# Layer 3 of a four-layer graph network: where the next batch's norm stands in VectorE's queue, and which block computes the first one

## The chip, the cores and the metric

The kernel runs on one core of one Trainium2 chip. The metric is the device time of one execution in microseconds (us). An execution is profiled once; it has a span, from its first to its last instruction, and some time around it.

## What is computed

Four layers share a residual: each takes h = relu(layernorm(x)) over 256 features, and adds its own result to x. Inputs are x (16 x 1024 x 256 values) and adj (16 x 1024 x 1024), in float32, read by the layers in other shapes of the same numbers. Layers 0 and 1 are dense graph layers. Layer 2 is a recurrence over nodes, which the kernel runs for all 16 batches at once. Layer 3, which the change is mostly about, is, cut to what matters:

```python
h = jnp.maximum(_layernorm(x, axis=-1), 0.0)
neighbor_sum = jnp.einsum('bnm,bmd->bnd', adjacency, h)
agg = epsilon * h + neighbor_sum
y = jnp.einsum('bnd,dh->bnh', agg, W1) + b1            # 256 -> 1024
y = jax.nn.silu(_rmsnorm(y, rms_weight))
out = jnp.einsum('bnh,hd->bnd', y, W2) + b2            # 1024 -> 256
x = x + out
```

## The kernel before

The names: a batch (b, 16 of them) has 1024 rows in 8 tiles of 128 (NT = 8), 256 features in two halves of 128 (DC = 2), 1024 hidden features in 8 pieces (HC = 8). Everything is float32.

Layers 0 and 1 run batch after batch and leave x in DRAM (x2_d). Layer 2 (layer_2, line 562 and on) walks over t = 0 to 7, one tile of 128 nodes of all 16 batches, and within it over s = 0 to 7, sub-steps of 16 nodes. A sub-step takes x from bxt and near (L970), runs round_ (L802 the matmuls, L843 and on the gates), turns the result (L870, L873) into h, and writes h with two indirect DMAs from GpSimd's queue to hs_d, one for each group of eight batches (L1034). Behind each sub-step stands a branch (tc.If, L1018) with repeats of the round for long chains of nodes. The recurrence is a chain: each sub-step needs the one before. In layer 2 the order of the instructions of TensorE, VectorE, ScalarE and GpSimd is the order in which the program writes them (manual_schedule); other work of the same block (L637, L687, L784, L749) is put between by hand. DMA issues of SP's queue are placed by the scheduler.

Before its last block, t = 7, the kernel calls early() (L919), which is early_3 (L1056): it starts the loads of batch 0 of layer 3: x[0], the first half of the transposed adjacency at[0][0], and the rows hn[0] of layer 2's result for tiles 0 to 6. They go into buffers of the pool "shared", which has two buffers of the name hb (x[0] and hn[0]) and two of the name bxt.

Layer 3 (layer_3, L1067) is not ordered by hand: a scheduler places the instructions of each engine at build time by the data they need and the buffers that are free, and may put later lines of the program ahead of earlier ones. For each batch there are these steps:

- load(b), L1093: x[b] (three buffers), hn[b] (layer 2's result, 7 tiles from hn_d and the last from hs_d; the two hb buffers), and at[b] in two halves of 512 columns, each in four pieces. Even batches use the two bxt buffers, odd ones two buffers named at. All are issued on SP's queue, which is first in, first out.
- prepare(b), L1108: GpSimd adds epsilon on the diagonal of at (L1112, four tiles for each half, with eye = epsilon times the unit matrix, L1088). VectorE adds hn[b] to x[b] (L1117, all eight tiles in one instruction but for batch 0) and calls ln_relu (L86): statistics for each tile (L92, L93), variance plus a constant (L79), GpSimd's power of -1/2 (L83), then for each tile VectorE's (x - mean) * rs into h[b] (L96) and ScalarE's Relu on it (L98). GpSimd adds b2 to x[b] (L1121). For batch 0 this is done in three parts, tiles 0 to 3, 4 to 6 and 7.
- sums(b), L1123: four parts of eight matmuls (L1130), one for each half of at and each half of the features; ScalarE or VectorE copies each result to ag (L1133, L1135). There are two pa buffers in PSUM.
- inner(ag, n0), L1138, for each half of the rows: for each of 8 pieces two matmuls into ph (L1145, two ph buffers in PSUM), ScalarE's square (L1148), VectorE's copy with b1 to hh (L1149), GpSimd's sum of the squares ss (L1151).
- norm: mean (L1163, four small matmuls, then L81 and L83), spread (L1169, four transposes into pr), apply (VectorE's hh * pr at L1174, ScalarE's Silu at L1175).
- outer(b, hh, n0), L1178: for each of four tiles eight matmuls into po (L1183, two po buffers) and VectorE's addition to x[b] (L1186).

A trace shows two matmul records for each float32 matmul of the program. The loop over batches at the end of layer_3 interleaves them: inner for both halves of b, two parts of sums(b + 1), outer for the first half, the third part of sums, prepare(b + 2), the fourth part, outer for the second half, and the output's DMA (L1217) from GpSimd's queue. prepare(b + 2) is written behind the third part, but in the built program the scheduler has put VectorE's part of it among the evictions of inner of the same batch b, for b = 2 to 13.

Of the kernel before, what the change touches and what calls it, by code (L numbers as in the profile page):

```python
# [40 lines left out]
def gnn_stack(ctx: ExitStack, tc: tile.TileContext, a: dict, out: bass.AP):  # L41
# [30 lines left out]
    def rows(ap):  # L72
        return ap.rearrange("(t p) d -> p t d", p=P)

    def inv_sqrt(pool, src, eps, shape, name, mul=1.0):
# [8 lines left out]
        return r  # L84

    def ln_relu(small, h, x):  # L86

        n = x.shape[1]
        mv = small.tile([P, NT, 2], F32, name="mv")
        for t in range(n):  # L90
            st = small.tile([P, 6], F32, name="st", bufs=4)
            nc.vector.bn_stats(st, x[:, t])  # L92
            nc.vector.bn_aggr(mv[:, t], st)  # L93
        rs = inv_sqrt(small, mv[:, :n, 1], LN_EPS, [P, n], "rs")
        for t in range(n):
            nc.vector.tensor_scalar(h[:, t], x[:, t], mv[:, t, 0:1], rs[:, t : t + 1],  # L96
                                    op0=ALU.subtract, op1=ALU.mult)
            nc.scalar.activation(h[:, t], h[:, t], AF.Relu)  # L98

# [462 lines left out]
    def layer_2(shared, early):  # L562
        with ExitStack() as st:
# [334 lines left out]
            with tc.manual_schedule(engines={mybir.EngineType.PE, mybir.EngineType.DVE, mybir.EngineType.Activation, mybir.EngineType.Pool}):  # L898
# [18 lines left out]
                for t in range(NT):  # L917
                    if t == NT - 1:
                        early()  # L919
                    base_todo = deque()  # L920
# [7 lines left out]
                    for s in range(NS):  # L928
# [68 lines left out]
                        for k, cut in enumerate(CUTS.get(s, ())):  # L997
# [11 lines left out]
                            if last:  # L1009
                                rx = round_(dx, xs, rx, cut, None, rest_if(False, 1.3), hT)  # L1010
                                turned(hT, rest_if(True, 0.5), h)
                            else:
                                rx = round_(dx, xs, rx, cut, hT, rest_if(False, 1.3), changes[cut])
                                dh = work.tile([P, G2, D], F32, name="dh", bufs=1)
                                turned(changes[cut], rest_if(False, 0.5), dh)
                                nc.gpsimd.tensor_tensor(from_(hT, cut), from_(hT, cut), from_(changes[cut], cut), ALU.add)
                        in_arms = gx.tasks if gx and s > 0 else ()
                        with tc.If(n_more[0][s] > 0, preferred_fallthrough_block=False) as more_or_not:  # L1018
# [25 lines left out]
                        elif t + 1 < NT:  # L1044
# [3 lines left out]
                            bxt, he = bxt_next, he_next  # L1048
                        sub = sub_next


# [3 lines left out]

    def early_3(shared, x, hn, at):  # L1056

        x[0] = shared.tile([P, NT, D], F32, name="hb")
        nc.sync.dma_start(x[0], rows(x2_d[0]))
# [4 lines left out]
        nc.sync.dma_start(hn[0][:, : NT - 2], rows(hn_d[0])[:, : NT - 2])  # L1064
        nc.sync.dma_start(hn[0][:, NT - 2], hs_d[NT - 2][0][:P])

    def layer_3(shared, x, hn, at):  # L1067
        with ExitStack() as st:
# [3 lines left out]
            psum = st.enter_context(tc.tile_pool(name="psum3", bufs=2, space=PSUM))  # L1072

            w1 = wp.tile([P, DC, H], F32, name="w1")
            nc.sync.dma_start(w1, a["W1"].rearrange("(c p) e -> p c e", p=P))
# [8 lines left out]
            nc.sync.dma_start(b2, bcast_row(a["b2"], D))  # L1084
            eps = wp.tile([P, 1], F32, name="eps")
            nc.sync.dma_start(eps, bcast_row(a["epsilon"], 1))
            eye = wp.tile([P, P], F32, name="eye")
            nc.vector.tensor_scalar(eye, ident, eps, None, op0=ALU.mult)  # L1088

            NH = 512  # L1090
            h = {}

            def load(b):  # L1093
                if b:
                    x[b] = big.tile([P, NT, D], F32, name="x", bufs=3)
                    nc.sync.dma_start(x[b], rows(x2_d[b]))
                    hn[b] = shared.tile([P, NT, D], F32, name="hb")
                    nc.sync.dma_start(hn[b][:, : NT - 1], rows(hn_d[b])[:, : NT - 1])
                    at[b] = []
                nc.sync.dma_start(hn[b][:, NT - 1], hs_d[NT - 1][b // GB][b % GB * P : (b % GB + 1) * P])  # L1100
                while len(at[b]) < N // NH:
# [6 lines left out]
            def prepare(b):  # L1108
                def diagonal(half):
                    for t in range(half * NT // 2, (half + 1) * NT // 2):  # L1110
                        own = at[b][half][:, t, t * P % NH : t * P % NH + P]
                        nc.gpsimd.tensor_tensor(own, own, eye, ALU.add)  # L1112
                diagonal(0)
                h[b] = big.tile([P, NT, D], F32, name="h", bufs=2)
                for part in ((0, NT),) if b else ((0, 4), (4, NT - 1), (NT - 1, NT)):
                    part = slice(*part)
                    nc.vector.tensor_add(x[b][:, part], x[b][:, part], hn[b][:, part])  # L1117
                    ln_relu(small, h[b][:, part], x[b][:, part])
                diagonal(1)
# [58 lines left out]
            def outer(b, hh, n0, apply=None):  # L1178
                for k in range(NH // P):
# [15 lines left out]
            for b in range(B):  # L1195
# [24 lines left out]
    with tc.tile_pool(name="shared", bufs=2) as shared:  # L1220
        x, hn, at = {}, {}, {}
        layer_2(shared, lambda: early_3(shared, x, hn, at))
        layer_3(shared, x, hn, at)

# [45 lines left out]
```

## Time and profile before

| what | us |
|---|---|
| median of three runs (4855.44 to 4871.58) | 4860.91 |
| the profiled execution | 4861.04 |
| its span | 4858.2 |
| TensorE busy with matmuls | 4494.9 (93%) |
| VectorE busy | 2303.1 (47%) |
| first matmul of layer 3 (L1130) starts at | 3418.39 |
| first ph matmul (L1145) of batch 0 starts at | 3447.76 |
| first ph matmul of batch 1 starts at | 3542.76 |

Times of single instructions are counted from the span's start. A row of the timeline gives start, length, engine, line, operation, output and inputs, how many instructions it merges, and in square brackets how long the engine stood idle before them and what ended that. A row of groups gives after the first bar the busy time and the mean length of one in ns, after the second bar the idle time just before them and what ended most of it. A row of the chain of waits gives start, length and what the path went through; "issue" is time in which nothing shown was waited for. PE is TensorE, DVE VectorE, ACT ScalarE, POOL GpSimd, SP the engine that issues most DMAs. A name in a row is the program's name of the buffer; batch 0's x and hn have the name hb.

### The profile page before, as it was taken

How to read it: one execution, taken by the hardware profiler on the slowest of the kernel's cores; microseconds unless marked ns; L12 is line 12 of the kernel's file. 1: busy time of each engine (PE TensorE's matmuls, PEld its weight loads, DVE VectorE, ACT ScalarE, POOL GpSimd, SP SyncE). 2: the span in 40 equal slices, each digit the busy share in tenths (PEclk: the TensorE clock that was granted, in tenths of full speed). 3: DMA queues.
4: the chain of work that ended last, by engine and by line, in shares of the span. 5: the costliest groups of instructions: out<-in, count | busy, mean ns of one | idle time of the engine just before them, and what ended most of it. 6: DMA issues, size and time to landing. Idle time of an engine off the chain costs nothing. (4 is left out here: it accounts for less than half of the span.)

```text
span 4858.2 us, 52472 instructions
## 1 busy us (share of the span) xinstructions
PE 4494.9 (93%) x18199; PEld 3004.6 (62%) x18199; DVE 2303.1 (47%) x6354; ACT 1220.2 (25%) x2629; POOL 1586.6 (33%) x1939
## 2 busy tenths in 40 slices
PE   8998899999997999999999999998899999999999
PEld 4443455555555777777777777776455555555556
DVE  6667854455543444444444444454534344344342
ACT  1211112222212222222322222222223223223232
POOL 3223233343323322332232323331534234243231
PEclk9999999999998999999999999998899999999999
DMA  4333235555537444444344544420422231222100
GB/s 157 113 99 104 88 88 183 194 165 176 184 104 209 149 137 133 149 142 149 115 140 122 157 139 153 142 82 29 169 87 70 78 104 65 91 88 78 70 26 18
DMA packets 530978, 576.61 MB, mean 119 GB/s; under 512 B 42544, under 2 KB 439472, under 8 KB 528304
## 3 DMA queue, kind: packets, MB, share of 16 engines
q1 hardware_dynamic: 499536, 460.27, 30.6%
q0 software_dynamic: 31040, 111.44, 6.4%
q8 instruction: 197, 3.23, 0.3%
q14 instruction: 205, 1.68, 0.1%
HBM read 469.65 MB, written 116.65 MB: 121 GB/s over the span
## 5 line engine op out<-in xcount | busy, mean ns | idle before, releaser
L309 PE MATMUL pa<-at,h 128*128 128x512 f32 x1088 | 497.4, 610 | 32.9 <-DVE ag L314 32.9
L1145 PE MATMUL ph<-ag,w 128*128 128x512 f32 x1024 | 478.3, 609 | 32.7 <-DVE hh L1149 32.4
L1183 PE MATMUL po<-w,hh 128*128 128x256 f32 x2048 | 447.7, 379 | 0.0
L637 PE MATMUL pf<-hb,ab 128*128 128x256 f32 x1568 | 420.6, 387 | 29.0 <-DVE bxt L787 16.2
L1183 PEld LDWEIGHTS po<-w,hh 128*128 128x128 f32 x2048 | 387.8, 190 | 59.3 <-issue 7.9
L309 PE MATMUL pa<-at,q 128*128 128x512 f32 x960 | 424.2, 595 | 0.0
L309 PEld LDWEIGHTS pa<-at,h 128*128 128x128 f32 x1088 | 209.9, 196 | 278.5 <-issue 232.8
L749 PE MATMUL pf<-hs,wx 128*128 128x256 f32 x1536 | 351.1, 383 | 16.6 <-POOL hs L740 14.9
L1145 PEld LDWEIGHTS ph<-ag,w 128*128 128x128 f32 x1024 | 178.6, 189 | 294.0 <-DVE hh L1149 151.4
L1151 POOL TENSOR_TENSOR ss<-ss,sq 128x512 f32<-128x512 f32 x224 | 304.9, 1361 | 118.7 <-ACT sq L1148 114.3
L749 PEld LDWEIGHTS pf<-hs,wx 128*128 128x128 f32 x1536 | 292.1, 192 | 60.1 <-POOL hs L740 16.8
L637 PEld LDWEIGHTS pf<-hb,ab 128*128 128x128 f32 x1568 | 278.2, 192 | 69.5 <-DVE bxt L787 23.4
L309 PEld LDWEIGHTS pa<-at,q 128*128 128x128 f32 x960 | 178.2, 190 | 216.1 <-issue 212.6
L1149 DVE TENSOR_SCALAR hh<-ph,b 128x512 f32<-128x512 f32 x256 | 189.8, 746 | 153.8 <-ACT sq L1148 120.5
L784 PE MATMUL pf<-bd,h 128*128 128x384 f32 (+5 forms) x768 | 214.4, 373 | 51.7 <-DVE bxt L787 26.5
L1034 POOL DMA_INDIRECT hs_d<-h,table x128 | 129.3, 1010 | 365.4 <-ACT gates L757 179.7
L1130 PE MATMUL pa<-bxt,h 128*128 128x512 f32 x512 | 227.9, 597 | 18.6 <-POOL bxt L1112 18.6
L1130 PE MATMUL pa<-at,h 128*128 128x512 f32 x512 | 228.8, 597 | 0.0
L1148 ACT ACTIVATE sq<-ph,b 128x512 f32<-128x512 f32 x224 | 153.6, 686 | 233.6 <-PE ph L1145 188.2
L787 DVE TENSOR_TENSOR bxt<-bxt,pf 128x384 f32<-128x384 f32 (+5 forms) x384 | 141.2, 384 | 149.1 <-PE pf L784 146.6
L1175 ACT ACTIVATE hh<-hh,rw 128x512 f32<-128x512 f32 x256 | 168.4, 712 | 138.5 <-DVE hh L1174 136.5
L754 DVE TENSOR_TENSOR gates<-pf,bias 128x512 f32<-128x512 f32 x128 | 88.4, 691 | 227.3 <-PE pf L749 227.3
(253 smaller groups left out, 7318.6 us busy)
## 6 DMA issues: line engine op xcount, KB each, us to landing
at<-in_adjT SPq DMA_DIRECT2D x64, 1024.0 KB, 7.2
ab<-in_adj SPq DMA_DIRECT2D x128, 512.0 KB, 4.0
bxt<-in_adjT SPq DMA_DIRECT2D x64, 512.0 KB, 5.8
at<-in_adjT SPq DMA_DIRECT2D x64, 512.0 KB, 5.8
ad<-in_adj SPq DMA_DIRECT2D x128, 128.0 KB, 6.0
x_d<-x POOLq DMA_DIRECT2D x16, 1024.0 KB, 5.4
he_d<-h POOLq DMA_DIRECT2D x16, 1024.0 KB, 9.5
heT_d<-hT POOLq DMA_DIRECT2D x16, 1024.0 KB, 4.4
```

The lines of the kernel that those rows point to most:

```text
L309: nc.tensor.matmul(pa, h[:, mt, c * P : (c + 1) * P], at[n0 // 512][:, mt], start=mt == 0, stop=mt == NT - 1)
L637: nc.tensor.matmul(pb, ab[:, jts[k]], hb[:, jts[k]], start=k == 0, stop=k == len(jts) - 1)
L749: nc.tensor.matmul(pg[:, e], wx[:, c, q * D + e * P : q * D + (e + 1) * P], self.hs[:, c], start=c == 0, stop=c == DC - 1)
L784: nc.tensor.matmul(pf, h[:, g, c * P : (c + 1) * P], bd[:, g, b4 : b4 + 4, S : S + far], start=True, stop=True)
L787: return lambda: nc.vector.tensor_add(to, to, pf)
L1130: nc.tensor.matmul(pa, h[b][:, mt, c * P : (c + 1) * P], at[b][n0 // NH][:, mt], start=mt == 0, stop=mt == NT - 1)
L1145: nc.tensor.matmul(ph, w1[:, c, k * P : (k + 1) * P], ag[:, c, n0 : n0 + NH], start=c == 0, stop=c == DC - 1)
L1148: nc.scalar.activation(sq, ph, AF.Square, bias=b1[:, k : k + 1])
L1149: nc.vector.tensor_scalar(hh[:, k], ph, b1[:, k : k + 1], None, op0=ALU.add)
L1151: nc.gpsimd.tensor_tensor(ss, ss, sq, ALU.add)
L1175: nc.scalar.activation(hh[:, k], hh[:, k], AF.Silu, scale=rw[:, k : k + 1])
L1183: nc.tensor.matmul(po, hh[:, c, k * P : (k + 1) * P], w2[:, c], start=c == 0, stop=c == HC - 1)
```

## The change

It has two parts.

In the batches of layer 3, prepare(b + 2) stands in a block tc.issue_after(last), where last is the fourth addition of outer's first half: each VectorE instruction of the block is ordered behind that addition. The addition of hn to x goes by two tiles at a time. The normalisation itself moves from VectorE to ScalarE: one small VectorE instruction makes shift = -mean * rs, and ScalarE's Relu takes shift as its bias and rs as its scale. VectorE's pass over each tile (L96) goes. The load of the last tile of hn stands directly behind that of the others.

For batch 0, early_3 becomes a generator whose steps layer_2 runs in its last block t = 7: the loads and that of epsilon ahead of the block; then, in one step each behind the rounds of s = 1, 2, 3 and 4: eye and tiles 0 to 2; tiles 3 to 5; tile 6, rs of the seven tiles and the diagonal of the first half; shift and the Relu of the seven tiles. Its small tiles lie in a pool of their own. h[0] is written into the buffer of hn[0]. Layer 3 starts with the load of tile 7 of hn[0] behind that of W1, and prepares only tile 7 and the second half's diagonal.

```diff
                     if t == NT - 1:
-                        early()
+                        eye = next(early)
...
+                        if t == NT - 1 and s > 0:
+                            next(early, None)
...
-    def early_3(shared, x, hn, at):
+    def early_3(shared, pool, x, hn, at, h):
+        eps = pool.tile([P, 1], F32, name="eps")
+        nc.sync.dma_start(eps, bcast_row(a["epsilon"], 1))
         x[0] = shared.tile([P, NT, D], F32, name="hb")
         nc.sync.dma_start(x[0], rows(x2_d[0]))
         at[0] = [shared.tile([P, NT, 512], F32, name="bxt")]
...
         hn[0] = shared.tile([P, NT, D], F32, name="hb")
         nc.sync.dma_start(hn[0][:, : NT - 2], rows(hn_d[0])[:, : NT - 2])
         nc.sync.dma_start(hn[0][:, NT - 2], hs_d[NT - 2][0][:P])
-
+        eye = pool.tile([P, P], F32, name="eye")
+        yield eye
+        n = NT - 1
+        nc.vector.tensor_scalar(eye, ident, eps, None, op0=ALU.mult)
+        mv = pool.tile([P, n, 2], F32, name="mv")
+        for t in range(n):
+            nc.vector.tensor_add(x[0][:, t], x[0][:, t], hn[0][:, t])
+            st = pool.tile([P, 6], F32, name="st", bufs=4)
+            nc.vector.bn_stats(st, x[0][:, t])
+            nc.vector.bn_aggr(mv[:, t], st)
+            if t % 3 == 2:
+                yield
+        rs = inv_sqrt(pool, mv[:, :, 1], LN_EPS, [P, n], "rs")
+        for t in range(NT // 2):
+            own = at[0][0][:, t, t * P : (t + 1) * P]
+            nc.gpsimd.tensor_tensor(own, own, eye, ALU.add)
+        yield
+        h[0] = hn[0]
+        shift = pool.tile([P, n], F32, name="shift")
+        nc.vector.scalar_tensor_tensor(shift, mv[:, :, 0], -1.0, rs, op0=ALU.mult, op1=ALU.mult)
+        for t in range(n):
+            nc.scalar.activation(h[0][:, t], x[0][:, t], AF.Relu, bias=shift[:, t : t + 1], scale=rs[:, t : t + 1])
+        yield
-    def layer_3(shared, x, hn, at):
+    def layer_3(shared, x, hn, at, h, eye):
...
+            nc.sync.dma_start(hn[0][:, NT - 1], hs_d[NT - 1][0][:P])
...
             def load(b):
                 if b:
...
                     nc.sync.dma_start(x[b], rows(x2_d[b]))
                     hn[b] = shared.tile([P, NT, D], F32, name="hb")
                     nc.sync.dma_start(hn[b][:, : NT - 1], rows(hn_d[b])[:, : NT - 1])
+                    nc.sync.dma_start(hn[b][:, NT - 1], hs_d[NT - 1][b // GB][b % GB * P : (b % GB + 1) * P])
                     at[b] = []
-                nc.sync.dma_start(hn[b][:, NT - 1], hs_d[NT - 1][b // GB][b % GB * P : (b % GB + 1) * P])
                 while len(at[b]) < N // NH:
                     n0 = NH * len(at[b])
                     half = shared.tile([P, NT, NH], F32, name="bxt") if b % 2 == 0 else big.tile([P, NT, NH], F32, name="at")
...
                     for t in range(half * NT // 2, (half + 1) * NT // 2):
                         own = at[b][half][:, t, t * P % NH : t * P % NH + P]
                         nc.gpsimd.tensor_tensor(own, own, eye, ALU.add)
-                diagonal(0)
-                h[b] = big.tile([P, NT, D], F32, name="h", bufs=2)
-                for part in ((0, NT),) if b else ((0, 4), (4, NT - 1), (NT - 1, NT)):
-                    part = slice(*part)
-                    nc.vector.tensor_add(x[b][:, part], x[b][:, part], hn[b][:, part])
-                    ln_relu(small, h[b][:, part], x[b][:, part])
+                part = slice(0 if b else NT - 1, NT)
+                if b:
+                    diagonal(0)
+                    h[b] = big.tile([P, NT, D], F32, name="h", bufs=2)
+                tiles = range(NT)[part]
+                mv = small.tile([P, NT, 2], F32, name="mv")
+                for t in tiles[::2]:
+                    two = slice(t, min(t + 2, NT))
+                    nc.vector.tensor_add(x[b][:, two], x[b][:, two], hn[b][:, two])
+                    for t in range(NT)[two]:
+                        st = small.tile([P, 6], F32, name="st", bufs=4)
+                        nc.vector.bn_stats(st, x[b][:, t])
+                        nc.vector.bn_aggr(mv[:, t], st)
+                n = len(tiles)
+                rs = inv_sqrt(small, mv[:, part, 1], LN_EPS, [P, n], "rs")
+                shift = small.tile([P, n], F32, name="shift")
+                nc.vector.scalar_tensor_tensor(shift, mv[:, part, 0], -1.0, rs, op0=ALU.mult, op1=ALU.mult)
+                for k, t in enumerate(tiles):
+                    nc.scalar.activation(h[b][:, t], x[b][:, t], AF.Relu, bias=shift[:, k : k + 1], scale=rs[:, k : k + 1])
                 diagonal(1)
...
-                    nc.vector.tensor_add(x[b][:, t], x[b][:, t], po)
+                    last = nc.vector.tensor_add(x[b][:, t], x[b][:, t], po)
+                return last.ins
...
-                outer(b, hh0, 0, apply1)
+                last = outer(b, hh0, 0, apply1)
                 parts[2]()
                 if b + 2 < B:
-                    prepare(b + 2)
+                    with tc.issue_after(last):
+                        prepare(b + 2)
                 parts[3]()
                 outer(b, hh1, NH)
```

ln_relu, which only layer 3 called, is removed. The other lines of the diff hand eye and h from function to function.

More of the change, by code (lines that the diff above doesn't have):

```diff
@@ L84, in inv_sqrt @@
         return r
[L86 to L98, printed above, removed]
     base_d = dram.tile([B, P, DC, P], F32, name="base_d")
@@ L1049, in layer_2 @@
                         sub = sub_next
-    def early_3(shared, x, hn, at):
+                return eye
+    def early_3(shared, pool, x, hn, at, h):
+        eps = pool.tile([P, 1], F32, name="eps")
+        nc.sync.dma_start(eps, bcast_row(a["epsilon"], 1))
         x[0] = shared.tile([P, NT, D], F32, name="hb")
@@ L1084, in layer_3 @@
             nc.sync.dma_start(b2, bcast_row(a["b2"], D))
[L1085 to L1088, printed above, removed]
             NH = 512
-            h = {}
             def load(b):
@@ L1220, in gnn_stack @@
     with tc.tile_pool(name="shared", bufs=2) as shared:
-        x, hn, at = {}, {}, {}
-        layer_2(shared, lambda: early_3(shared, x, hn, at))
-        layer_3(shared, x, hn, at)
+        x, hn, at, h = {}, {}, {}, {}
+        with tc.tile_pool(name="first3", bufs=1) as first:
+            eye = layer_2(shared, early_3(shared, first, x, hn, at, h))
+            layer_3(shared, x, hn, at, h, eye)
 def kernel(**inputs):
```

## The prediction

> **What bounds the kernel now.** I read the page first, then TensorE's idle time by line, then TensorE's and VectorE's timelines of one layer-3 batch, then the chain of waits where layer 2 turns into layer 3.
>
> ```profile
> PE 4494.9 (93%) x18199; PEld 3004.6 (62%) x18199; DVE 2303.1 (47%) x6354; ACT 1220.2 (25%) x2629; POOL 1586.6 (33%) x1939
> ...
> L1145 PE MATMUL ph<-ag,w 128*128 128x512 f32 x1024 | 478.3, 609 | 32.7 <-DVE hh L1149 32.4
> ```
>
> TensorE is the bound, and the change removes none of its matmuls, so it can only win TensorE's idle time. 32.4 us of it stand before the ph matmuls, waiting for VectorE's eviction hh. Cut at the first ph matmul of a batch, the stage table (stretch, its length, TensorE busy, clock, DMA share, GB/s) shows in which batches:
>
> ```profile
> 3542.76:3629.16 86.40, 86.31 (x282) 1.00 0.21 73
> 3629.16:3719.30 90.14, 85.69 (x274) 1.00 0.23 82
> 3719.30:4615.32 896.02, 872.48 (x2809) 1.00 0.23 81
> 4615.32:4704.77 89.45, 87.10 (x281) 1.00 0.07 24
> 4704.77:4790.87 86.10, 86.10 (x282) 1.00 0.03 13
> ```
>
> The first row is b = 1, the next three are b = 2 to 13, the last is b = 14. Twelve batches take 1075.61 us, 89.63 each; the two at the edges take 86.40 and 86.10. TensorE has the same matmuls in all; the twelve have a next batch's norm on VectorE among the evictions of hh, the two have none. TensorE and VectorE in one of the twelve:
>
> ```profile
> 4012.01 1.98 PE L1145 MATMUL ph<-ag,w 128*128 128x512 f32 x4 [0.37 <-DVE hh L1149]
> ...
> 4014.97 1.99 PE L1145 MATMUL ph<-ag,w 128*128 128x512 f32 x4 [0.87 <-DVE hh L1149]
> ...
> 4019.78 1.98 PE L1145 MATMUL ph<-ag,w 128*128 128x512 f32 x4 [0.68 <-DVE hh L1149]
> ...
> 4023.06 1.98 PE L1145 MATMUL ph<-ag,w 128*128 128x512 f32 x4 [0.44 <-DVE hh L1149]
> ```
>
> ```profile
> 4011.87 2.39 DVE L96 TENSOR_SCALAR h<-x,mv,rs 128x256 f32<-128x256 f32 x4
> 4014.18 0.74 DVE L1149 TENSOR_SCALAR hh<-ph,b 128x512 f32<-128x512 f32 x1
> 4014.84 1.56 DVE L96 TENSOR_SCALAR h<-x,mv,rs 128x256 f32<-128x256 f32 x2
> ```
>
> Four and two normalisations stand ahead of one eviction each; TensorE, with two ph buffers, stops. At the change of layers the chain shows the second loss:
>
> ```profile
> 3402.06 6.03 DMA hs_d<-h,table
> ...
> 3414.76 2.27 DVE h L96 x3
> 3417.03 0.68 DVE eye L1088
> 3417.70 0.07 issue
> 3417.77 0.58 POOL bxt L1112
> 3418.35 0.04 issue
> 3418.39 29.54 PE pa L1130 x64
> ```
>
> TensorE's last transpose of layer 2 ends at 3399.75; batch 0's sums start 18.64 us later, behind the write of h, the norm, eye and the diagonal.
>
> **What the skill says.** "TensorE: Matmul & The Clock Gate", the section on the array's architecture, says that ScalarE's and VectorE's queues are strictly first in, first out. The lines above agree: an eviction whose ph is ready waits 2.39 us behind normalisations. "ScalarE: Activation LUTs", section What ACT_TABLE_LOAD costs, prices each pointer operand (scale, bias) at about 93 ns over an immediate one; here a 128x256 Relu with immediates takes 415 ns (L98), one with both pointers 589 (below), so 87 each: it agrees. I use 589, and 0.50 us apart in a row (589 less the skill's overlap of 93, an estimate).
>
> ```profile
> L301 ACT ACTIVATE h<-x,shift,rs 128x256 f32<-128x256 f32 x128 | 64.7, 589 | 16.6 <-DVE shift L298 16.6
> ```
>
> **Part 1, layer 3's batches.** The built order of after puts all of prepare(b+2) on VectorE between the 4th and the 5th x addition of outer, for b = 0 to 13. Per batch 8 normalisations at 0.648 = 5.2 us go from VectorE; ScalarE's 8 Relu at 0.415 become 8 at 0.589; one tiny shift (0.16) is added. ph's matmuls now run 20, 6, 4, 2 with mean and spread between, as b = 1 and 14 do today, and VectorE's list there is that of b = 1. So I take 86.25 (mean of the two) for all fourteen: 12 x (89.63 - 86.25) = **40.6 us gained**. Bounds: 36 (0.4 us per batch left) to 42.4 (all at 86.10).
> Cover in the new place, on the clock of the batch above: the 4th x addition ends at 4051.8. VectorE then needs 4 additions of two tiles (2.34 in one piece at L1117, so about 2.5), statistics 3.4 (3426.47 to 3429.83 for batch 1), rs_v 0.2; GpSimd's pow 1.65 and two hand-overs 0.3; shift 0.2: done near 4060.2. Queued behind shift are the ag copy, whose pa is ready at 4065.1, and outer's second half, first due 4068.4. Nothing waits. On ScalarE one Relu now stands before the ag copy of 4058.26, which slips to about 4061; its reader is the next batch at 4078. The other seven end near 4065, in 22 us of idle time. GpSimd's x + b2 (8 x 0.77) and four diagonals end near 4073, before the out DMA (4079.66). If that cover were gone, each us of lateness beyond the slack costs 14 us in all.
> DMAs: on SP's queue hn[b+3] now stands between the two halves of at[b+3] and waits for prepare(b+2)'s additions. It lands in 5.1 us after issue, some 80 us before use; x[b+2], issued at 3995.00, is used at 4052. Cost nothing.
>
> **Part 2, batch 0 ahead of time.** In after, tiles 0 to 6, eye, and the first half's diagonal are done in t = 7. The built order of TensorE is 7 matmuls of one sum, 2 of the next, then the one with tile 7. They start when the last h copy is read out, 3400.5 (was 3418.4). 32 matmuls took 29.53 us, 0.92 each, so 9 end at 3408.8. Tile 7: the write of group 0 is issued at 3400.77. In t = 7 such writes land after 2.5 to 2.8 us; here the write of group 1 took 6.03 beside w1 and w2. In after only w1 runs beside it, so I take 4.5: 3405.3. Its load, moved ahead of w2, takes 2.4 to 3: 3408. Addition, statistics, rs_v 1.2, pow 0.6 + 0.2, shift 0.2, Relu 0.6: 3410.7. Stall 1.9 (0 to 6.5). The sums end at 3400.5 + 29.5 + 1.9 = 3431.9 against 3447.9: **16.0 gained** (11.5 to 17.9).
> What is late next is batch 1. h[0] now lies in hn[0]'s buffer, so hn[1] loads only after batch 0's sums (before: issued 3418.05): 3432 + 5.1, and with more behind it about 3437.5. VectorE's two additions for x[1] stand behind two evictions; behind them stand the third eviction and all later ones. Additions and statistics 5.9, so the third eviction is at 3443.3 to 3444.0; TensorE, done with four ph at 3439, idles 5.0. Then 8 Relu (4.0) before the fifth square on ScalarE: idle 4.1; GpSimd's x + b2 (6.1) before the squares' sums: 1.1 more. 10.2 in all over an undisturbed 86.3, so 96.5. Batch 0 took 3542.76 - 3447.76 = 95.0 with its own stalls: **1.5 lost** (4 gained to 7 lost).
>
> **Part 3, layer 2's last block.** Before, two of these additions stand in its first sub-step:
>
> ```profile
> 3207.40 0.96 DVE L1117 TENSOR_TENSOR hb<-hb 128x768 f32<-128x768 f32 x1 [5.40 <-DMA hb<-hs_d]
> 3209.34 2.78 PE L802 MATMUL pc<-r,wh 128*128 128x256 f32 x8 [2.43 <-DVE r L844]
> ```
>
> VectorE waits for a DMA with r behind it, TensorE for r: 2.43, and 0.40 for x behind the first addition: **2.8 gained** (0 if other fillers eat it). Added: in s = 1 and 2 three tiles (0.42 + 0.40 + 0.16 each, 2.9) and eye (0.74), in s = 3 one tile. VectorE idles 2.97 us there in s = 1, 3.04 in s = 2, until the gates' sums; up to 0.7 over, before the second gate eviction, with 0.97 of idle behind it. ScalarE's 7 Relu in s = 4 (3.6) delay a gate eviction by 2; TensorE reads its result over 2 us later. GpSimd's pow and four diagonals (2.8) in s = 3 delay the write of h, whose reader is far. I take nothing, up to 3.
>
> **Sum.** 40.6 + 16.0 - 1.5 + 2.8 = 57.9. The profiled execution took 4861.0 (span 4858.2 and 2.8 around it), within 0.2 us of the median 4860.9. 4861 - 58 = **4803**.
>
> **Rivals.** (a) The change of layers gives little: hn[1] lands late, tile 7 lands after 6 us, the recurrence pays 3: 40.6 + 11.5 - 7 - 3 + 0 = 42, so 4819. For it: VectorE's queue is blocked by a load there for the first time. Against: five us of slack counted already. (b) The stalls don't go with the norm: only VectorE's multiplications by pr hold ph back. Then 16.0 - 1.5 + 2.8 = 17 remains: 4844. For it: 0.68 and 0.44 of the four waits stand among those multiplications. Against: b = 1 and 14 have them too and no wait. (c) Slower: shift waits for GpSimd's pow, which stands behind four diagonals that wait for at[b+2]; today GpSimd waits 101.6 us for at loads (18 times, longest 28.6). The slack to the third po is 4071.4 - 4060.2 = 11 us; each us beyond costs 14, so above 11 + 58/14 = 15 us it is slower than before. At 20 us late: 9 x 14 = 126 - 58, so 4929. Against: in after's order those diagonals are on a half loaded a batch earlier.
>
> **How the numbers follow.** My forecast 0.75, (a) 0.14, (b) 0.06, (c) 0.03, more gain than all the bounds 0.02. All best: 42.4 + 17.9 + 4 + 2.8 = 67, so 4794; (a) reaches 4819, and with 36 in place of 40.6 for the batches 4824. 0.3% is 14.6 us, about what a measurement of this kernel can tell from no change. (b)'s 17 lies just above it, half of it counted as no change: faster 0.94, same 0.03, slower 0.03.
>
> **What would show it.** Right: batches 1 to 14 each near 86.2 us and no [<-DVE hh] waits there; VectorE's shift ahead of the ag copy; batch 0's first sum directly behind layer 2's last transpose; a VectorE wait on hn[1] with TensorE idle near 5 and 4 us behind it. Wrong: batches near 89, TensorE waiting for x additions in outer, a sub-step of t = 7 longer than before.

## The result, and the profile after

The kernel after takes 4802.57 us (median of four runs, 4794.02 to 4806.04) against 4860.06 (four runs, 4855.44 to 4871.58): ratio 0.9872, 95% interval 0.9856 to 0.9888. Its profiled execution took 4804.16, the forecast was 4803.

Of the page after I show the lines that answer to those of before: TensorE's and VectorE's busy time, and the group of the ph matmuls (now L1170), whose idle time <-DVE hh has gone from 32.4 to 8.3 us.

```profile
PE 4482.4 (93%) x18199; PEld 3004.1 (63%) x18199; DVE 2250.0 (47%) x6292; ACT 1238.4 (26%) x2629; POOL 1561.7 (33%) x1938
...
L1170 PE MATMUL ph<-ag,w 128*128 128x512 f32 x1024 | 467.3, 607 | 8.4 <-DVE hh L1174 8.3
```

The stage table, cut at the first ph matmul of a batch: b = 1, b = 2 to 13, b = 14, and last b = 0. Behind the stretch stand its length, then busy time and number of records of TensorE, of its weight loads, of VectorE, ScalarE and GpSimd, then the granted clock, the DMA share and GB/s.

```profile
3529.32:3615.42 86.10, 86.10 (x281) 50.38 (x280) 32.31 (x66) 26.22 (x42) 31.48 (x34) 1.00 0.26 86
3615.42:4648.90 1033.48, 1033.41 (x3362) 604.61 (x3361) 387.62 (x792) 314.64 (x504) 373.41 (x400) 1.00 0.23 80
4648.90:4735.00 86.10, 86.10 (x282) 50.38 (x281) 26.33 (x44) 22.28 (x34) 20.72 (x17) 1.00 0.04 13
3432.51:3529.32 96.81, 88.24 (x281) 51.11 (x280) 39.39 (x88) 31.17 (x51) 41.83 (x50) 0.96 0.38 130
```

TensorE is busy for 1033.41 us of 1033.48: the twelve batches take 86.12 each and it is idle for 0.07 us in all of them. VectorE in one of them, from outer's fourth addition on:

```profile
4018.58 0.42 DVE L1211 TENSOR_TENSOR x<-x,po 128x256 f32<-128x256 f32 x1 [3.03 <-PE po L1208]
...
4026.60 0.17 DVE L1141 SCALAR_TENSOR_TENSOR shift<-mv,rs 128x8 f32<-128x8 f32 x1 [1.76 <-POOL rs L83]
4032.31 0.69 DVE L1160 COPY ag<-pa 128x512 f32<-128x512 f32 x1 [5.54 <-PE pa L1155]
```

Shift ends 7.8 us behind the addition, and the ag copy behind it still waits 5.54 for TensorE. What is left stands in batch 0. TensorE from the end of layer 2 on:

```profile
3401.66 9.69 PE L1155 MATMUL pa<-bxt,hb 128*128 128x512 f32 x18 [0.79 <-ACTq L1008]
3412.66 20.01 PE L1155 MATMUL pa<-bxt,hb 128*128 128x512 f32 x46 [1.31 <-ACT hb L1143]
3432.51 7.14 PE L1170 MATMUL ph<-ag,w 128*128 128x512 f32 x16
3446.08 5.46 PE L1170 MATMUL ph<-ag,w 128*128 128x512 f32 x8 [6.43 <-DVE hh L1174]
3451.38 1.02 PE L1155 MATMUL pa<-at,h 128*128 128x512 f32 x2
3454.26 7.31 PE L1170 MATMUL ph<-ag,w 128*128 128x512 f32 x16 [1.86 <-DVE hh L1174]
```

VectorE in the same time: two evictions, then batch 1's addition, which waits for the load of hn[1], and only behind the statistics the third eviction.

```profile
3436.86 0.75 DVE L1174 TENSOR_SCALAR hh<-ph,b 128x512 f32<-128x512 f32 x1 [0.97 <-ACT sq L1173]
3438.53 2.36 DVE L1133 TENSOR_TENSOR x<-x,hb 128x512 f32<-128x512 f32 x2 [0.92 <-DMA hb<-hn_d]
...
3445.32 0.71 DVE L1174 TENSOR_SCALAR hh<-ph,b 128x512 f32<-128x512 f32 x1
```

The balance of the two profiled executions, before less after: batches 1 to 14 1248.11 - 1205.68 = 42.4; from the issue of layer 2's last pair of writes to the first ph 46.99 - 30.62 = 16.4; batch 0 -1.8; the block t = 7 203.9 - 201.7 = 2.2; everything ahead of t = 7, where the programs do the same work, -3.3; behind the last batch boundary -0.1. Before rounding they add up to 55.7, the difference of the spans, 4858.2 - 4802.5.

### The profile page after: what moved, and what is told of

It reads as the page before. It is cut to its first block, busy times and chain, and to the rows that moved or that the text cites. A ratio compares the mean times of both kernels' runs of the same rounds, so it can differ in the third digit from the quotient of the medians.

```text
span 4802.5 us, 52444 instructions
## 1 busy us (share of the span) xinstructions
PE 4482.4 (93%) x18199; PEld 3004.1 (63%) x18199; DVE 2250.0 (47%) x6292; ACT 1238.4 (26%) x2629; POOL 1561.7 (33%) x1938
## 3 DMA queue, kind: packets, MB, share of 16 engines
q1 hardware_dynamic: 499536, 460.27, 30.8%
## 5 line engine op out<-in xcount | busy, mean ns | idle before, releaser
L1170 PE MATMUL ph<-ag,w 128*128 128x512 f32 x1024 | 467.3, 607 | 8.4 <-DVE hh L1174 8.3
L1170 PEld LDWEIGHTS ph<-ag,w 128*128 128x128 f32 x1024 | 179.8, 190 | 259.5 <-issue 146.5
L1176 POOL TENSOR_TENSOR ss<-ss,sq 128x512 f32<-128x512 f32 x224 | 284.6, 1271 | 149.9 <-ACT sq L1173 149.4
L83 POOL TENSOR_TENSOR rs<-rs_v,mhalf 128x8 f32<-128x8 f32 (+1 forms) x65 | 106.9, 1644 | 346.0 <-DVE rs_v L79 332.5
L1155 PE MATMUL pa<-bxt,h 128*128 128x512 f32 x448 | 197.4, 593 | 0.0
```

Source lines behind the costliest of these rows:

```text
L1155: nc.tensor.matmul(pa, h[b][:, mt, c * P : (c + 1) * P], at[b][n0 // NH][:, mt], start=mt == 0, stop=mt == NT - 1)
L1170: nc.tensor.matmul(ph, w1[:, c, k * P : (k + 1) * P], ag[:, c, n0 : n0 + NH], start=c == 0, stop=c == DC - 1)
L1176: nc.gpsimd.tensor_tensor(ss, ss, sq, ALU.add)
```

## The experiments

The theory: TensorE lost its time to the place of the norm in VectorE's queue, so the order alone wins the batches; batch 0 stalls because h[0] holds hn[1]'s buffer. The main rival: the gain is VectorE's pass that was moved to ScalarE. All runs in one table; t7 is the block t = 7, "change" the time from the issue of layer 2's last pair of writes to the first ph, b0 batch 0, b1-14 the mean of batches 1 to 14, all from the profiled execution; ratio to the kernel before as run beside it on the same chip, with its 95% interval (its median there was 4856.3 to 4860.1).

| kernel | t7 | change | b0 | b1-14 | median us | ratio |
|---|---|---|---|---|---|---|
| before | 203.9 | 47.0 | 95.0 | 89.15 | 4860.1 | 1 |
| after | 201.7 | 30.6 | 96.8 | 86.12 | 4802.6 | 0.9872 (0.9856 to 0.9888) |
| order_only | 204.7 | 46.6 | 86.0 | 86.12 | 4810.8 | 0.990 (0.9879 to 0.9921) |
| fuse_only | 201.6 | 30.6 | 101.5 | 91.31 | 4879.8 | 1.004 (1.0023 to 1.0057) |
| ahead_only | 201.1 | 30.6 | 102.8 | 89.51 | 4851.6 | 0.9988 (0.9981 to 0.9996) |
| fuse_x4 | 198.9 | 30.8 | 102.0 | 90.84 | 4872.7 | 1.0034 (1.0021 to 1.0046) |
| before_x4 | 203.8 | 47.0 | 96.0 | 86.45 | 4821.9 | 0.9934 (0.9911 to 0.9957) |
| stats_x3 | 201.1 | 32.3 | 96.2 | 86.12 | 4800.1 | 0.9884 (0.9867 to 0.9900) |
| stats_x6 | 201.6 | 30.6 | see below | see below | 4798.6 | 0.988 (0.9863 to 0.9898) |
| hn1_free | 201.4 | 30.6 | 86.7 | 86.12 | 4783.5 | 0.9858 (0.9836 to 0.9881) |
| hn1_w1 | 199.0 | 36.0 | 86.0 | 86.11 | 4791.5 | 0.9866 (0.9850 to 0.9883) |
| hn1_w1b | 201.8 | 29.0 | 86.0 | 86.12 | 4788.6 | 0.9858 (0.9836 to 0.9879) |
| steps_late | 198.8 | 30.8 | 96.9 | 86.10 | 4793.7 | 0.9868 (0.9847 to 0.9889) |
| after_again | 199.3 | 30.8 | 96.7 | 86.12 | 4800.5 | 0.988 (0.9860 to 0.9900) |

The block t = 7 begins between 3189.3 and 3200.2 in these traces, although what runs before it is the same work in all: 11 us that no edit explains. So small effects are read from the stages, not from the totals.

### The order alone (order_only)

```diff
-                    nc.vector.tensor_add(x[b][:, t], x[b][:, t], po)
+                    last = nc.vector.tensor_add(x[b][:, t], x[b][:, t], po)
+                return last.ins
...
-                outer(b, hh0, 0, apply1)
+                last = outer(b, hh0, 0, apply1)
...
-                    prepare(b + 2)
+                    with tc.issue_after(last):
+                        prepare(b + 2)
```

> The kernel before with one thing changed: prepare(b + 2) stands behind the fourth addition of outer's first half. VectorE still does the eight normalisations, 5.2 us a batch. Theory 'place': what cost TensorE time was where the norm stood in VectorE's queue, not how long it is. The normalisations then end about 4031.3 on the clock of the batch of after that I looked at (4026.6 when rs is there, plus 8 x 0.58), and the next instruction with a reader, the ag copy, is first due at 4031.6: just hidden. Batches 2 to 13 near 86.2 each in place of 89.63, total near 4861 - 42 = 4819. Rival 'work': the gain comes from VectorE's pass that went to ScalarE, so that without it most of the stalls come back in the new place: batches near 89, total over 4845.

Measured: 4810.8, batches 1 to 14 at 86.12 as after. VectorE still does all the normalisations; its busy time is even 2320.7. In one batch, VectorE's timeline behind the fourth addition:

```profile
4026.94 2.28 DVE L1117 TENSOR_TENSOR x<-x,hb 128x2048 f32<-128x2048 f32 x1
...
4032.62 0.17 DVE L79 TENSOR_SCALAR rs_v<-mv 128x8 f32<-128x8 f32 x1
4034.55 5.14 DVE L96 TENSOR_SCALAR h<-x,mv,rs 128x256 f32<-128x256 f32 x8 [1.76 <-POOL rs L83]
4040.33 0.69 DVE L1135 COPY ag<-pa 128x512 f32<-128x512 f32 x1 [0.65 <-PE pa L1130]
```

The wait for pow and all eight normalisations end 0.65 us before the ag copy can start. The page's ph group says the same in one number:

```profile
L1145 PE MATMUL ph<-ag,w 128*128 128x512 f32 x1024 | 465.3, 605 | 0.2 <-DVE hh L1149 0.2
```

What I had not expected is batch 0 at 86.0 in place of 95.0: prepare(2) had stood in it too. That is why the total is 8 below the expected 4819.

### The norm on ScalarE alone (fuse_only)

```diff
-                    with tc.issue_after(last):
-                        prepare(b + 2)
+                    prepare(b + 2)
```

(against after)

> The kernel after without the block that orders prepare(b + 2) behind the last addition; the normalisation stays on ScalarE. The built order has VectorE's additions, statistics and shift among the evictions of inner again. Theory 'place': part of the stalls stays, since shift waits for GpSimd's pow (1.65 us and two hand-overs) with evictions behind it, and up to 2.6 us of additions and statistics stand ahead of one: batches near 88, so about 12 x 1.9 = 23 us more than after, near 4826. Rival 'work': without the eight normalisations what stands among the evictions fits into VectorE's 1.03 us of idle time before each, so batches near 86.2 and a total as after, 4803.

Measured: 4879.8, slower than before. The rival is refuted, and the theory's size was too small: batches 2 to 13 take 92.2 on average, where before has 89.6. One batch of it, VectorE and then GpSimd and TensorE at the same moment:

```profile
4104.96 0.17 DVE L79 TENSOR_SCALAR rs_v<-mv 128x8 f32<-128x8 f32 x1
4106.88 1.22 DVE L1141 SCALAR_TENSOR_TENSOR shift<-mv,rs 128x8 f32<-128x8 f32 x1 [1.75 <-POOL rs L83]
4108.03 0.74 DVE L1174 TENSOR_SCALAR hh<-ph,b 128x512 f32<-128x512 f32 x1
```

```profile
4105.21 1.64 POOL L83 TENSOR_TENSOR rs<-rs_v,mhalf 128x8 f32<-128x8 f32 x1 [1.51 <-DVE rs_v L79]
4106.82 1.25 POOL L1176 TENSOR_TENSOR ss<-ss,sq 128x512 f32<-128x512 f32 x1
```

```profile
4108.82 1.98 PE L1170 MATMUL ph<-ag,w 128*128 128x512 f32 x4 [2.01 <-DVE hh L1174]
```

VectorE waits 1.75 us for pow, and then the tiny shift itself takes 1.22, just until GpSimd's sum of squares ends. In 12 of 15 batches shift lies beside such a sum and takes 1.22; in the other three no GpSimd instruction runs and it takes 0.17, as in after. Behind it stands an eviction, and TensorE stops for 2.01. (It waits 1.02 more behind VectorE's addition, which waits 0.83 for x's load, and 0.84 for GpSimd's sum of squares.) The Trainium skill, page "SBUF — State Buffer", section "SBUF: two separate sides", says that a VectorE instruction with two SBUF inputs and a GpSimd instruction that reads SBUF lock each other out of one port pair for the whole instruction; shift has two (mean and rs), and the trace agrees. In after's place GpSimd has no sum of squares to do, and shift takes 0.17.

The one-tensor normalisation of before is not spared. Its first five in a batch take 0.40 to 0.41 each; the sixth starts together with a sum of squares of 1.26 and takes 1.42, and the last two, beside GpSimd's additions of b2, 0.83 and 0.81. Over before's batches 1 to 15 the lengths in ns (least, median, most) are:

```profile
L96 DVE TENSOR_SCALAR h<-x,mv,rs x120: 400/412/1421, 3431.8 to 4641.6; 128x256 f32<-128x256 f32 x120
```

Why the form with one tensor is held up as well, no run here shows.

The waits are not all of fuse_only's loss. Two neighbouring batches, and a part of the first:

```profile
3990.27:4082.30 92.03, 88.18 (x282) 51.23 (x281) 34.11 (x66) 26.04 (x42) 31.82 (x34) 0.98 0.23 80
4082.30:4173.05 90.75, 86.76 (x282) 50.50 (x281) 34.10 (x66) 25.83 (x42) 31.90 (x34) 1.00 0.24 81
4018.12:4021.54 3.42, 3.42 (x7) 1.67 (x6) 1.50 (x2) 3.25 (x7) 3.42 (x6) 0.50 0.00 0
```

Both have the stop of 2.01 and are idle for about 3.9 in all, but in the first the granted clock is half for 3.4 us just behind that stop, and TensorE is busy for 1.4 longer. Nine of the twelve batches have one such stretch, the slowest (95.4) two, and the two at 90.7 none; order_only, where TensorE hardly waits, has a clock of 1.00 from batch 1 to batch 14.

### Batch 0 ahead alone (ahead_only)

```diff
-                tiles = range(NT)[part]
...
-                for k, t in enumerate(tiles):
-                    nc.scalar.activation(h[b][:, t], x[b][:, t], AF.Relu, bias=shift[:, k : k + 1], scale=rs[:, k : k + 1])
+                nc.vector.tensor_add(x[b][:, part], x[b][:, part], hn[b][:, part])
+                ln_relu(small, h[b][:, part], x[b][:, part])
...
-                    with tc.issue_after(last):
-                        prepare(b + 2)
+                    prepare(b + 2)
```

(ln_relu of before is back; not shown)

> The kernel after with the norm of batches 1 to 15 as in the kernel before (one addition, VectorE's normalisation, no order): only batch 0's norm in the recurrence's last block and tile 7's load ahead are left. Theory: the two parts of the change add up, so it gains 16.4 at the change of layers and 2.2 in the last block, less 2 to 7 in batch 0, whose late hn[1] now also has the normalisations of batch 1 behind it: total 4846 to 4851, batches 2 to 13 at 89.6 as before. Rival: the parts are not apart (moving the loads of hn on SP's queue ahead of at's second half is what freed the batches): batches near 87.5, total near 4825.

Measured: 4851.6, 4.7 under the kernel before as run beside it (4856.3), less than half of the expected gain of 10 to 15. The change of layers gains its 16.4 and the last block 2.7, but batch 0 loses 7.8 to the late hn[1] with normalisations behind it, and batches 1 to 14 lose 5.0. In one of those batches VectorE's order and TensorE's waits are those of before, but VectorE waits 0.92 for x's load where it waited 0.48, and TensorE 0.17 more behind that; what makes that load later is not settled. The rival, faster batches, did not come.

### A fourth buffer for x (fuse_x4 and before_x4)

```diff
-                    x[b] = big.tile([P, NT, D], F32, name="x", bufs=3)
+                    x[b] = big.tile([P, NT, D], F32, name="x", bufs=4)
```

(fuse_x4 makes this edit in fuse_only, before_x4 in before.)

> The kernel after without the block that orders prepare(b + 2), with four buffers for x in place of three. Without the order the batches took 92.1, more than before's 89.5. Two waits of VectorE were seen among the evictions there: 0.83 for the load of x[b+2], which starts only when the output of b - 1 has left its buffer, and 1.75 for GpSimd's pow ahead of shift. VectorE's order is nearly the same here, but the load of x[b+2] has a free buffer. Theory: both waits count alike, so the first of TensorE's two waits (1.02) goes and the second (2.01) stays: batches near 90.8, total near 4862. Rival 1: all comes from the late x: batches 86.2, total near 4800. Rival 2: the load has no part in it: 92.1, total 4880.

Measured: 4872.7, batches 2 to 13 at 92 but for the first at 95.4, two near 90.4 and the last at 86.1. It doesn't tell what it was meant to: SP's queue still waits 197 us in all for the output's writes ahead of x's loads (before: 210), and VectorE still waits 0.76 to 1.06 for x in batches 3 to 12. The two near 90.4 are no answer to the question either: they have the same stop of 2.01, but a granted clock of 1.00 where their neighbours have 0.98. How much of fuse_only's loss is x's late load stays open.

> The kernel before with four buffers for x in layer 3 in place of three; nothing else is edited. The load of x[b+2] may still come late, as it did with four buffers and the normalisation on ScalarE. But the built order of VectorE is another: the addition, the statistics and rs_v stay among the evictions of inner, and the eight normalisations stand behind the ag copy and ahead of outer's last four additions. Theory 'place': what waits for GpSimd's pow and what follows it does the harm among the evictions, the addition and the statistics (2.3 us at most in one piece) do not: batches near 86.4, total near 4861 - 40 = 4821. Rival: the late x and the statistics hold evictions up as well: batches 87.5 to 89, total 4835 to 4855.

Measured: 4821.9, batches 3 to 14 at 86.1, as the theory had it (batch 2 takes 91.1, with VectorE waiting 3.0 for x's load; before has 2.8 there). This build has the addition, the statistics and rs_v among the evictions, and x is as late as before; only what needs pow stands elsewhere. Its VectorE:

```profile
3984.59 2.30 DVE L1117 TENSOR_TENSOR x<-x,hb 128x2048 f32<-128x2048 f32 x1 [0.47 <-DMA x<-x_d]
3986.82 1.40 DVE L1149 TENSOR_SCALAR hh<-ph,b 128x512 f32<-128x512 f32 x2
...
3992.74 0.16 DVE L79 TENSOR_SCALAR rs_v<-mv 128x8 f32<-128x8 f32 x1
3994.10 0.16 DVE L81 TENSOR_SCALAR rms_v<-pq 128x4 f32<-128x4 f32 x1 [1.20 <-PE pq L1163]
3994.18 0.74 DVE L1149 TENSOR_SCALAR hh<-ph,b 128x512 f32<-128x512 f32 x1
```

So of before's norm it was the wait for pow and the eight normalisations behind it that held TensorE up; 2.3 us of addition and 3.4 of statistics among the evictions did not. GpSimd's additions of b2, which follow the normalisations, moved with them, and beside GpSimd a normalisation takes two to three and a half times its 0.41: how much of the harm was VectorE's own work and how much its waiting for GpSimd is not separated.

### How much cover the new place has (stats_x3 and stats_x6)

```diff
+                if b > 1:
+                    for _ in range(2):
+                        for t in tiles:
+                            st = small.tile([P, 6], F32, name="st", bufs=4)
+                            nc.vector.bn_stats(st, x[b][:, t])
+                            nc.vector.bn_aggr(mv[:, t], st)
```

(range(5) in the second)

> The kernel after with the eight statistics of each prepare(b), b from 2 on, computed three times over (the last result is the one used): 16 more pairs of bn_stats and bn_aggr, 6.8 us of VectorE, between the fourth addition of outer's first half and shift. Theory: the place has slack. In after, shift ends at 4026.8 of the batch from 3960, the first addition behind it is due at 4035.8 and TensorE needs its result at 4039.0; shift at 33.5 delays the ag copy by 1.5 us, which nobody awaits. Batches 86.1, total near 4803. Rival: VectorE's time counts here too, since ScalarE's Relu and GpSimd's x + b2 come later: 14 x up to 6.8 us, total 4830 to 4898.

Measured: 4800.1, batches at 86.12; the rival is out.

> As the run with the statistics three times over, but six times: 17 us more on VectorE in front of rs_v. Theory: now the slack of some 12 us to TensorE's third po is used up. In the built order the ag copy and the first addition of outer's second half stand just ahead of the last bn_aggr; they end near 4042.5 on that clock, 3.5 us after TensorE needs them: 14 x 3.5 = 49 us over after, near 4852. The recorded prediction's own rule, 14 us for each us beyond 11, gives 14 x 6 = 84, near 4887. Rival: VectorE's queue is refilled freely and nothing waits: 4803.

Measured: 4798.6. Both numbers that I had worked out, 4852 and 4887, are wrong for this kernel. The added 40 pairs take 0.39 each, 15.6 us, and shift does end late. But the scheduler knew of it and built another order for TensorE:

```profile
4014.24 13.90 PE L1161 MATMUL pa<-at,h 128*128 128x512 f32 x32
4027.98 7.07 PE L1214 MATMUL po<-w,hh 128*128 128x256 f32 x32
4034.89 2.74 PE L1176 MATMUL ph<-ag,w 128*128 128x512 f32 x6
4037.46 7.07 PE L1214 MATMUL po<-w,hh 128*128 128x256 f32 x32
```

Between the second and the third po stand six matmul records of the next batch's ph. Batches 0 to 14 take 1305.4 in all against after's 1302.5, with 14 x 15.6 = 218 us more of VectorE in them.

### hn[1] in a free buffer, and W1 later (hn1_free, hn1_w1, hn1_w1b)

```diff
-                    hn[b] = shared.tile([P, NT, D], F32, name="hb")
+                    hn[b] = (big.tile([P, NT, D], F32, name="h", bufs=2) if b == 1
+                             else shared.tile([P, NT, D], F32, name="hb"))
```

> The kernel after with hn[1] in a buffer of the name h of layer 3, which is free then, in place of the buffer that h[0] holds until batch 0's sums end. Its load then stands ahead of at[1] on SP's queue and lands near 3427, and the built order has all of batch 1's norm on VectorE between the two ag copies, ahead of batch 0's first eviction. Theory: the two stalls of batch 0 in after, 6.43 and 1.86 us, come from the late load alone: batch 0 near 88.5 in place of 96.8, total near 4795. Rival: the loads of layer 3's start take turns anyway (w1, w2, x[1], at[1], 5 MB), so at[1] or x[1] is then late: batch 0 at 94 or more, or batch 1 longer, total 4800 to 4805.

Measured: batch 0 86.7, total 4783.5. Both stalls came from the buffer: of 6.43 and 1.86 a single wait of 0.48 is left, and the loads taking turns cost no more than that. The total is 11 below the expected 4795, of which batch 0 explains 1.8; in this trace the block t = 7 begins 10.9 earlier than in after's, behind work that the edit doesn't touch.

The other two add, for W1 and W2, and in hn1_w1b for b2 too:

```diff
-            nc.sync.dma_start(hn[0][:, NT - 1], hs_d[NT - 1][0][:P])
+            tile7 = nc.sync.dma_start(hn[0][:, NT - 1], hs_d[NT - 1][0][:P])
...
+            with tc.issue_after(tile7.ins):
                 nc.sync.dma_start(w1, a["W1"].rearrange("(c p) e -> p c e", p=P))
```

> The kernel after with hn[1] in a buffer of the name h, and W1 and W2 ordered behind the load of tile 7 of hn[0], so that the last writes of layer 2's h to DRAM and that load have the DMA engines to themselves. Theory: the write lands in 2.5 to 2.8 us as in the recurrence, in place of 5.4, tile 7's h is there near 8.5 us after the write's issue, and TensorE's stall of 1.3 us in batch 0's first sum goes; W1 still lands before its first use 23 us later. Batch 0 as with hn[1] free, total 4782. Rival: the landing time is not due to W1 (it would stay 5.4, the stall 1.3 us), or W1 is late and the first ph waits: total 4785 or more.

Measured: 4791.5, the change of layers 36.0, worse by 5.4. The first half of the theory held: the write landed 2.9 us after its issue (3392.70, the load behind it issued at 3395.58). But GpSimd's queue was built in another order:

```profile
3399.36 4.99 POOL L1149 TENSOR_TENSOR hb<-hb,b 128x256 f32<-128x256 f32 x7 [4.39 <-DMA b<-in_b]
3404.31 0.58 POOL L83 TENSOR_TENSOR rs<-rs_v,mhalf 128x1 f32<-128x1 f32 x1
```

Seven additions of b2 stand ahead of tile 7's pow, because b2 now loads early, and TensorE waits 4.51 us.

> As the kernel with hn[1] in a buffer of the name h and W1 and W2 behind the load of tile 7, with the load of b2 behind it too. In the first form the last write of h landed 2.9 us after its issue in place of 5.5, as expected, but GpSimd's additions of b2 had come ahead of the pow for tile 7 in its queue and cost TensorE 4.5 us; here the built order has the pow first. Theory: tile 7's load, which now runs beside W1, W2 and x[1], takes 3.9 in place of 2.1, so h's last tile is there 0.8 us earlier than with W1 first, and the stall in batch 0's first sum is 0.5 in place of 1.25. Batch 0 at 86.1 to 86.7. Total about 1 below the kernel with hn[1] free, 4783 to 4790. Rival: nothing is gained over it.

Measured: with b2 loaded late the pow is first, and batch 0's sums run in one piece:

```profile
3391.73 29.39 PE L1159 MATMUL pa<-bxt,hb 128*128 128x512 f32 x64 [0.79 <-ACTq L1008]
3420.95 17.97 PE L1174 MATMUL ph<-ag,w 128*128 128x512 f32 x40
```

The change of layers takes 29.0, batch 0 86.0. The total, 4788.6, is not below hn1_free's 4783.5 on another chip; the change of layers is 1.6 shorter (30.6 to 29.0), less than totals can show.

> The kernel after, once more, beside the version with hn[1] free and W1 later. Theory: 4803, batch 0 at 96.8, and about 11 us above that version: 10.2 for batch 0 and 0.8 for tile 7. Rival: the layers before differ by several us from one execution to the next, so that the two can't be told apart.

Measured: 4800.5 beside hn1_w1b's 4788.6 on the same chip, 12 us, where the stages give 10.7 for batch 0 and 1.8 for the change of layers. The intervals of the two ratios (0.9860 to 0.9900 and 0.9836 to 0.9879) overlap by about half, so the totals alone don't part the two; batch 0 does, at 96.2 to 96.9 in four traces with hn[1] behind h[0] in after's order and at 86.0 to 86.7 in three with it in a free buffer. By that stage hn1_free and hn1_w1b beat after, and by their totals before.

### The early norm's steps later (steps_late)

```diff
-                        if t == NT - 1 and s > 0:
+                        if t == NT - 1 and s > 2:
                             next(early, None)
```

> The kernel after with the four steps of batch 0's early norm behind the rounds of s = 3, 4, 5 and 6 of the last block in place of s = 1 to 4. In eight traces with the early norm, s = 2 took 1.5 us more than before, and s = 3 and 4 together 1.9 more, s = 1 0.2 more; s = 5 to 7 gave about 1.5 back. Theory: the steps cost what they take where they stand, so s = 1 and 2 go back to 16.6 and 17.3, and s = 3 to 6 get 3 to 4 us longer; the block as a whole stays near 201.4, total near 4803. Rival: the later sub-steps have idle time on VectorE that hides them, the block takes 198 and the total is 4800; or the last Relu come too late for batch 0's first sum, and TensorE waits there.

Measured: s = 1 to 4 take 67.6, after 70.7 and before 66.9; s = 5 and 6 together get 1.5 longer than before, and s = 7, where no step stands, is 3.1 shorter. The block takes 198.8, the lowest of all, but the ten with the steps behind s = 1 to 4 spread from 198.9 to 201.8, so one trace doesn't settle it. Batch 0's first sum waits 1.52 for tile 7 (after: 1.31): the Relu come in time.

## Why the prediction was right, by its steps

- **Part 1, batches.** 40.6 was forecast, 42.4 came, the upper bound: the batches ran at 86.1, the better of the two that I had averaged. The mechanism, the norm among the evictions, is shown by order_only and before_x4. The prediction did not say which half of the edit does it: it is the order, and the pass to ScalarE is worth nothing there; without the order it costs. Two readings were off without harm: the 0.648 of a normalisation is not VectorE's own work but 0.41 with waiting for GpSimd in it, and the cut at 3719.30 lies 1.6 ahead of batch 3's first ph (3720.91), which leaves the sum of the twelve as it is.
- **Its cover.** Nothing was late: from the fourth addition's end to shift's 8.4 were forecast and 7.8 came, and TensorE's idle time in b = 2 to 13 is 0.07 us. So rival (c) did not come: the diagonals ahead of pow in GpSimd's queue were done 14 us before it, and shift waits 1.76, for pow alone. The rule "each us beyond costs 14", on which (c)'s threshold rests, could not be tested by stats_x6, since the build knew of the late work and filled TensorE's time; what a lateness costs that a build does not foresee stays open.
- **Part 2, ahead of time.** 16.0 forecast, 16.4 measured. The write took 5.4 us beside W1 in place of 4.5, yet the stall was 1.3 in place of 1.9, since the first matmuls ran slower (18 records in 9.69 us, 0.54 each against 0.43 for the 46 behind), so that tile 7 was needed later. The granted clock is 0.82 in those 9.69 us and 1.00 behind; the first 9.61 us of before's sums have 0.81, so the mean of 0.92 a matmul hid a slow start that was there to be read. With W1's load behind it the write landed in 2.9 (hn1_w1), so it is W1's traffic that the landing waits for. What the early norm and the earlier load of tile 7 are worth apart, no run shows.
- **Batch 0.** 96.5 forecast, 96.8 measured. The parts were less good: 6.43, 1.86 and 0.28 in place of 5.0, 4.1 and 1.1. The eight Relu took the forecast 4.0, but the second stall is shorter, in part because two matmul records of batch 1's sums (1.02) stand in it; and TensorE's busy time is 2.1 over an undisturbed batch, which I had not counted: the granted clock is half for 6.8 us there, from 3442.83 to 3449.66. That the total came within 0.3 is luck. The cause, hn[1] behind h[0], is shown by hn1_free. What I missed: without that buffer batch 0 was worth another 9 to 10 us, since prepare(2) left it as well.
- **Part 3, t = 7.** 2.8 forecast; 203.9, the median of three traces without the early steps, against 201.3 in ten with them: 2.6. But the terms are other ones: s = 0 gains 3.9 to 5.7, not 2.8; s = 1 to 4 lose about 3.5, where I took nothing (up to 3); s = 5 to 7 give about 2 back. The sum is right by luck.
- **The sum.** 57.9 forecast, 57.5 between the medians. The profiled executions differ by 56.9, and they would differ by 3.3 more, had the time ahead of t = 7 not been longer by that, in work that the change doesn't touch. The four stages together gained 59.2; that the forecast met the total within 0.4 us is luck.
- **Rival (a)** needed hn[1] and tile 7 late and the recurrence to pay 3: tile 7's stall was 1.3, the block gained. **Rival (b)** is refuted by order_only: the multiplications by pr are all there, and the wait for hh is 0.2.

## What to carry to other kernels

Ask of each instruction in a queue that feeds the bound engine whether it waits for a third engine: 5.7 us of addition and statistics among the evictions cost nothing (before_x4), while the pow wait and what hangs on it cost 3.4 us a batch (batches 3 to 13: 89.44 in before, 86.07 in before_x4). Move the place first and the work second; work moved to another engine but left in the wrong place made batches 1 to 14 30 us longer (fuse_only, 1278.3 against 1248.1). When a new lifetime is put into an old buffer, look for the next load into it: a name with a free buffer won 10 us.

## What was not expected of the hardware

- A VectorE instruction of 128x8 took 1218 ns in place of 168 beside GpSimd's sum of squares (fuse_only), and a normalisation of one tensor of 128x256 took 1.42 us in place of 0.41 beside such a sum (before).
- A stall costs TensorE more than its idle time: in fuse_only the ph matmuls wait 49.6 us, and their busy time is 488.2 against 465.3 in order_only, 23 us more for the same matmuls. Some 16 us of it (an estimate: nine batches with 1.4 and one with 3.1 more busy time than the two at full clock) go with stretches of half the granted clock behind stops of 2 us and more; two batches had the same stop of 2.01 and no such stretch, so a stop of that length doesn't always bring it.
- The indirect write of h landed in 2.9 us with only small loads beside it (hn1_w1), and in 5.4 beside the 1 MB of W1 (after).
- Layer 3's first matmuls, behind the recurrence, ran at a granted clock of 0.82 for 9.69 us and then at 1.00 (after); in before it was 0.81 for 9.61 us.
